# Where a position table is cast during attention, and how its products are ordered, in a two-layer image kernel

## The chip, the cores and the metric

The kernel runs on one core of a Trainium2 chip. The metric is device time in microseconds (us) of one execution. Three runs of the kernel before gave 2399.17, 2401.52 and 2405.88; their median, 2401.52, is the time before.

The engines are named as in the profile: PE (TensorE, the matrix products; PEld are its weight loads), DVE (VectorE), ACT (ScalarE), POOL (GpSimd) and SP (SyncE, which here issues DMAs only).

## The reference

Eight images of 32 x 32 tokens with 384 channels go through two layers. Layer 0 is group normalisation, attention with six heads of 64 channels over the 1,024 tokens of an image, a projection and a residual. To the logits it adds relative positions, taken apart into rows and columns:

```
attn  = einsum('bqd,bkd->bqk', q * SCALE, k)
rel_h = einsum('bhwc,hkc->bhwk', r_q, Rh)      # r_q: q as (heads, 32, 32, 64)
rel_w = einsum('bhwc,wkc->bhwk', r_q, Rw)
attn  = attn(b, h, w, h', w') + rel_h[..., None] + rel_w[..., None, :]
out   = softmax(attn) @ v @ proj_w + proj_b
```

Layer 1 is a layer norm with causal single-head attention and a residual, and then a feed-forward: a layer norm, a matrix of signs, a quantisation to 8 bits (clip of `y * 128 / (max|y| + eps)`) over a group of images, gelu, another matrix of signs, another such quantisation, and a residual. Eight images in five groups make groups of one image, so images 0 to 4 pass through the feed-forward and images 5 to 7 get zeros from it.

## The kernel before

**Order of the work.** The images are done one after the other in the order 5, 0, 1, 2, 3, 4, 6, 7. Each engine executes its own list of instructions, one after the other. A scheduler makes these lists when the program is built: it starts from the order of the Python code and may move work forward whose inputs and buffers are there earlier. The helper `tc.issue_after(ins)` keeps what is issued inside its block behind the instruction `ins`. PSUM tiles come from a pool of eight banks (`o_tile`), pages in SBUF from a pool of twelve (`page`) and larger tiles from a pool of eleven (`image`, `flat`).

**Start of an image, `layer0`.** Six calls of `queries_keys(m)` make q (m = 0 to 2, one for each pair of heads) and k (m = 3 to 5). Each is two halves of three 128x512 matmuls (`f_qk`, L438); ACT takes the first half out of PSUM (L468), DVE the second (L466). The table products belong to q: `positions(p)` multiplies q of pair p with the relative table (`f_rel`, L484, two halves of two matmuls); ACT copies the row part out of PSUM (L489), DVE the column part (L490); SP writes both to DRAM (`far`, L496) and reads them back as a shifted table of the pair (`near`, L501). In the kernel before, `positions(m - 1)` follows `queries_keys(m)` for m = 1, 2 and 3, so that a product, a projection, a product, a projection alternate. After m = 3 the last piece of the previous image's feed-forward is issued (`unfinished.pop()()`, the function `finish`), and then come k of pairs 1 and 2 and the eight tiles of v (`f_v`, L534; ACT and DVE copy them out, L537).

An image that follows one with a feed-forward (five do: 1, 2, 3, 4 and 6) has its first two projections, m = 0 and m = 1, computed ahead of time, inside that feed-forward (`ahead`, `project_qk`). Its start is therefore `f_rel` and `f_qk` of m = 2. The end of the feed-forward lies beside it: DVE finds the scale `qs` and the limits `qu` and `ql` (L946, L948), POOL clips eight tiles (L950), and DVE adds them scaled to `f_x` (L954, eight); these additions are part of `finish`, so in the Python code they follow m = 3 and `positions(2)`.

**Casting a table, `place(p)`.** The shifted table of a pair is split into a rounded part and a remainder so that the matmul can use both: ACT casts (`hi`, L514), DVE subtracts (`lo`, L515), twice each per pair (rows, then columns). Sixteen DMAs then put the parts into the four operands `r` (L522), eight of them issued by SP (`hi`) and eight by POOL (`lo`). In the kernel before `place` is a generator with one stop, between rows and columns. `place(0)` runs whole before attention; `place(1)` and `place(2)` are drawn from the generator `others` within attention.

**Attention, `attend0_fast`.** Six rounds go through (p, half) = (0,0), (0,1), (1,0), (1,1), (2,0), (2,1). In a round

- PE makes eight tiles of scores, each from two products q k (L590) and two products of a unit matrix with `r` (L594);
- ACT takes two exponentials of each tile (L600);
- DVE adds the eight tiles up, once L605 and six times L607 (`add_up`), then transposes and reduces (`over_tiles`, L624, L626);
- PE multiplies the exponentials with v (`f_av`, L615), and ACT copies the result out (L662);
- for the round before, PE makes the denominators (`f_den`, L633), DVE takes reciprocals (L637), sums both for a check on the values (`seen`, L427, L428; the last readers of the PSUM bank) and spreads them (L641, L642), and POOL multiplies (L659). This stands behind the sixth addition of DVE (`late_add`, `adds[4]`).

In the third round (1,0) `residual` loads the image again (SP, L106) and POOL adds a bias to its eight tiles (L569). In rounds 1 and 2 (p = 0) the kernel before draws two steps each from `later`, which puts a whole `place` into each of them:

```
if p == 0:
    with tc.issue_after(last_exp[0]):
        for _ in range(2):
            next(later, None)
```

Here `last_exp[0]` is the last exponential of the round on ACT; the subtractions on DVE are issued in the same block.

**First image only.** Image 5 also prepares the feed-forward's weights: `binarize`, called in round 5, loads them in pieces (POOL's DMAs, L232), and DVE sums them (L250). The scheduler moves the start of this forward: in the trace the first load is issued at 99.98 and the first sum starts at 106.6, ahead of the third round.

Of the kernel before, what the change touches and what calls it, by code (L numbers as in the profile page):

```python
# [11 lines left out]
F32 = mybir.dt.float32  # L12
# [3 lines left out]
ALU = mybir.AluOpType  # L16
# [9 lines left out]
NPAIR = NH // 2  # L26
# [49 lines left out]
def conv_attn_hybrid(  # L76
# [19 lines left out]
    nc = tc.nc  # L96
# [197 lines left out]
    def multiply_out(pools):  # L294
        both = pools.flat("wqkT")
        wqT_sb, wkT_sb = (both[:, i * NC * C : (i + 1) * NC * C].rearrange("p (k c) -> p k c", k=NC) for i in range(2))
        nc.sync.dma_start(out=wqT_sb, in_=wqT.rearrange("(k p) c -> p k c", p=P))
        nc.sync.dma_start(out=wkT_sb, in_=wkT.rearrange("(k p) c -> p k c", p=P))
        for m in range(NC):
            ps = pools.o_tile(f"wqk_{m}")  # L300
            for k in range(NC):
                nc.tensor.matmul(ps[:, :C], wqT_sb[:, k, ts(m, P)], wkT_sb[:, k, :], start=(k == 0), stop=(k == NC - 1))
            nc.vector.tensor_scalar_mul(wqk[:, m, :], ps[:, :C], C**-0.5)

    def stages(pools):
# [137 lines left out]
        def layer0(b, xT):  # L443
# [9 lines left out]
            def queries_keys(m):  # L453
                p = m % NPAIR
                bias = bqk[:, m : m + 1]
                made = ahead.pop((b, m)) if (b, m) in ahead else project_qk(b, xT, m)
                for half, ps in enumerate(made):
                    t = ts(half, 512)
                    if m < NPAIR:
                        dst = q[:, p, t]  # L460
                    else:
                        dst = k[:, p, t].rearrange("d (g n i) -> d g i n", n=2, i=P)
                        ps = ps.rearrange("d (g i n) -> d g i n", n=2, i=P)
                    scale = qscale if m < NPAIR else 1.0
                    if half:
                        nc.vector.tensor_scalar(dst, ps, scale, bias, ALU.mult, ALU.add)  # L466
                    else:
                        nc.scalar.activation(dst, ps, AF.Identity, bias=bias, scale=scale)  # L468
# [5 lines left out]
            def positions(p):  # L474

                if p < 1:
                    *pages, near = (pools.page(f"{n}_{b}_{p}") for n in ("far0", "far1", "near"))
                else:
                    room = pools.flat(f"far_{b}_{p}")
                    *pages, near = (room[:, ts(i, T)] for i in range(3))  # L480
                for half in range(2):
                    ps = [pools.o_tile(f"rel_{b}_{p}_{half}_{par}") for par in range(2)]
                    for par in range(2):
                        nc.tensor.matmul(  # L484
                            ps[par], rel[rows[par]].rearrange("d a n -> d (a n)"), q[rows[par], p, ts(half, 512)],
                            start=True, stop=True,
                        )
                    for par in range(2):
                        nc.scalar.copy(pages[par][:HD, ts(half, 512)], ps[par][:HD])  # L489
                        nc.vector.tensor_copy(  # L490
                            pages[par].rearrange("i (w h) -> i w h", h=H)[HD:, :, ts(half, H // 2)],
                            ps[par][HD:].rearrange("i (h w) -> i w h", w=W),
                        )
                for par in range(2):
                    far = store.tile([P, T], F32, tag=f"far_{p}_{par}", bufs=2, name=f"{pools.path}_far_{b}_{p}_{par}")
                    nc.sync.dma_start(out=far, in_=pages[par])  # L496
                    start = far[0:1, 0:1]
                    for d in range(2):
                        for half in range(2):
                            at, step = (d * HD + (half if d else 16 * half)) * T, (2 if d else 1) * T  # L500
                            nc.sync.dma_start(  # L501
                                out=near[ts(4 * d + 2 * half + par, 16)].rearrange("m (n o) -> m n o", n=32),
                                in_=bass.AP(start.tensor, start.offset + at, [[step, 16], [T + 32, 32], [1, 32]]),
                            )
                return near, [page.bitcast(F32R) for page in pages]

            def place(p, near, pages):


                for d in range(2):  # L510
                    hi, lo, src = (t[ts(d, HD)].rearrange("k (h w) -> k h w", h=H) for t in (*pages, near))
                    if d:
                        src = near[ts(d, HD)].rearrange("k (w h) -> k h w", h=H)
                    nc.scalar.copy(hi, src)  # L514
                    nc.vector.tensor_tensor(lo, src, hi.bitcast(F32), ALU.subtract)  # L515
                    if d == 0:
                        yield
                for part in range(4):
                    for d in range(2):
                        for i in range(2):  # L520
                            half = part % 2 if d else part // 2
                            (nc.gpsimd if i else nc.sync).dma_start(  # L522
                                out=r[part][:, p, :].bitcast(F32).rearrange("(m i) t -> i m t", i=4)[2 * i + d],
                                in_=pages[i][ts(2 * d + 1 - half, 32)].bitcast(F32),
                            )
# [13 lines left out]
            near = []  # L539
            for m in range(2 * NPAIR):  # L540
                queries_keys(m)
                if 0 < m <= NPAIR:
                    near.append(positions(m - 1))
                if m == NPAIR and unfinished:
                    unfinished.pop()()

                    early = pools.small.tile([P, 1], F32, tag="early", name=f"early0_{b}")
                    nc.scalar.activation(early, k[:, 0, T - 1 :], AF.Exp, scale=0.0)
            for j in range(NJ):
                values(j)  # L550
            r.extend(pools.image(f"r_{b}_{part}", F32R) for part in range(4))
            for _ in place(0, *near[0]):
                pass

            def others():
                for p in range(1, NPAIR):
                    yield from place(p, *near[p])
                    yield

            later = others()  # L560
            for _ in () if pools.fast else later:
                pass
            if pools.fast and b == ORDER[0]:
                join_biases(pools)

# [8 lines left out]
        def attend0_fast(residual, b, q, k, r, v, later):  # L574
# [5 lines left out]
            last_exp, last_matmul = [None], [None]  # L580
# [22 lines left out]
            def add_up(p, half, prs):  # L603
                total = pools.page(f"sum0_{b}_{p}_{half}")
                adds = [nc.vector.tensor_tensor(total, prs[0], prs[1], ALU.add).ins]  # L605
                for pr in prs[2:]:
                    adds.append(nc.vector.tensor_tensor(total, total, pr, ALU.add).ins)  # L607
                return total, adds[4]

            def values(p, half, prs):  # L610
                av = pools.o_tile(f"av0_{b}_{p}_{half}")
# [34 lines left out]
            for p, half in itertools.product(range(NPAIR), range(2)):  # L646
                t, last = ts(half, 512), (p, half) == (NPAIR - 1, 1)
                prs = [scores(p, c, half) for c in range(NJ)]
                if b == ORDER[0] and (p, half) == (0, 0):
                    multiply_out(pools)  # L650
                if b == ORDER[0] and (p, half) == (2, 0):
                    signs.append(binarize(pools))
                    next(signs[0])
                total, late_add = add_up(p, half, prs)
                if waiting is not None:
                    p0, t0 = waiting[0], ts(waiting[1], 512)
                    with tc.issue_after(late_add):
                        rb = reciprocals(*waiting)
                    (nc.vector if last else nc.gpsimd).tensor_tensor(oT[:, p0, t0], oT[:, p0, t0], rb, ALU.mult)  # L659
                av = values(p, half, prs)  # L660
                if not last:
                    nc.scalar.copy(oT[:, p, t], av)  # L662
                if (p, half) == (1, 0):
                    xt = residual()
                if p == 0:
                    with tc.issue_after(last_exp[0]):
                        for _ in range(2):
                            next(later, None)
                waiting = (p, half, over_tiles(p, half, total))
            nc.vector.tensor_tensor(oT[:, p, t], av, reciprocals(*waiting), ALU.mult)  # L670
            with behind_last():
# [334 lines left out]
    with ExitStack() as scope:  # L1006
        pools = Pools(scope, tc, "f")
# [43 lines left out]
```

## Time and profile before

| | us |
|---|---|
| time before, median of three runs | 2401.52 |
| profiled execution, its own time | 2400.84 |
| profiled execution, span from first to last instruction | 2399.1 |
| mean granted TensorE clock in it | 0.992 |
| L590, q k scores: 1536 matmuls | 423.8 busy, 27.3 idle before |
| L607, additions: 288, mean 1311 ns | 377.4 busy, 17.8 idle before |
| L514, casts: 32, mean 1532 ns | 49.0 busy, 0.8 idle before |
| L515, subtractions: 32, mean 1770 ns | 56.6 busy, 47.5 idle before |
| L490, DVE's copies of products: 96, mean 692 ns | 61.8 busy, 13.1 idle before |
| L569, POOL's bias additions: 64, mean 1728 ns | 108.8 busy, 50.0 idle before |

How to read this: "busy" is the sum over all instructions of that line; "idle before" is the time in which the engine stood just before one of them. Idle time of an engine counts only if the chain that sets the end passes through it. Each line of code has one row for each engine and shape, so a row's count tells over how many images or rounds it is spread: 32 subtractions are four for each image, those of pairs 1 and 2; those of pair 0 stand in a row of their own.

The profile gives times in microseconds from the start of the span. In its tables of stretches, a row holds the stretch, its length, then the busy time of PE, PEld, DVE, ACT and POOL with the number of instructions, the granted clock, the DMA share and GB/s.

### The profile page before, as it was taken

The page shows a single profiled execution, that of the slowest core. Times are in us where ns is not written, and L with a number is a line of the kernel's source. Part 1 is how long each engine was busy: PE and PEld are TensorE (multiplying, and loading weights), DVE is VectorE, ACT ScalarE, POOL GpSimd, SP SyncE. Part 2 cuts the span into 40 slices and gives each one's busy share as a digit, 9 for nine tenths or more (in the row PEclk, how much of TensorE's full clock was granted, in tenths as well). Part 3 has the DMA queues.
Part 4 walks back from the last instruction along what each step waited for, and adds up shares of the span by engine and source line. Part 5 has one row for each costly group of instructions (what it writes and reads, how often), then busy time and mean ns, then how long its engine had stood idle before and what let it go on. Part 6 is the DMA issues. An engine that isn't in the chain of part 4 may idle for free.

```text
span 2399.1 us, 26120 instructions
## 1 busy us (share of the span) xinstructions
PE 2347.1 (98%) x9442; PEld 1311.2 (55%) x9442; DVE 1441.9 (60%) x2302; ACT 1041.7 (43%) x1763; POOL 329.9 (14%) x421
## 2 busy tenths in 40 slices
PE   7899999999999999999999999999999999999998
PEld 3445544558644577445684455864457744554454
DVE  4585558655587347684455864558734668524851
ACT  3451155227463246551375522746424655115520
POOL 0310014000240001410002300024000131001300
PEclk9999999999999999999999999999999999999999
DMA  6610371220631012510108211053101271017100
GB/s 165 191 39 25 151 145 47 79 79 1 141 97 66 1 40 83 145 43 34 40 4 174 60 66 40 1 133 105 53 14 40 69 151 44 1 50 153 36 1 28
DMA packets 154795, 169.99 MB, mean 71 GB/s; under 512 B 113408, under 2 KB 126048, under 8 KB 153120
## 3 DMA queue, kind: packets, MB, share of 16 engines
q1 hardware_dynamic: 134416, 98.93, 16.4%
q0 software_dynamic: 17184, 69.22, 9.7%
q8 instruction: 77, 1.26, 0.2%
q10 hardware_dynamic: 3056, 0.08, 0.1%
q14 instruction: 62, 0.51, 0.1%
HBM read 75.38 MB, written 42.47 MB: 49 GB/s over the span
## 4 chain that ended last, share of the span: by engine, by line
PE 90%; DVE 5%; DMA 3%; SPq 1%; issue 1%; ACT 0%; POOL 0%; DVEq 0%; ACTq 0%
PE f_s L590 12%; PE f_av L615 11%; PE f_qk L438 10%; PE f_s L779 8%; PE f_av L792 8%; PE f_y L940 7%; PE f_y L899 7%; PE f_pj L386 5%; PE f_v L386 5%; PE f_q L738 5%; PE f_v L534 5%; PE f_s L594 4%; DVE f_sum L607 3%; PE f_rel L484 2%; DMA f_x<-in_x 1%; PE f_pt L314 1%
## 5 line engine op out<-in xcount | busy, mean ns | idle before, releaser
L600 ACT ACTIVATE f_pr<-f_s 128x512 f32<-128x512 f32 x768 | 413.5, 595 | 103.7 <-PE f_s L594 87.4
L590 PE MATMUL f_s<-f_q,f_k 64*128 64x512 f32 x1536 | 423.8, 611 | 27.3 <-DVE seen L427 27.3
L607 DVE TENSOR_TENSOR f_sum<-f_sum,f_pr 128x1024 f32<-128x1024 f32 x288 | 377.4, 1311 | 17.8 <-ACT f_pr L600 0.9
L615 PE MATMUL f_av<-f_pr,f_v 128*64 128x512 f32 x1536 | 339.3, 594 | 0.0
L594 PE MATMUL f_s<-f_r,unit 64*128 64x512 f32 x768 | 329.2, 808 | 0.2 <-DMA f_r<-f_far 0.2
L438 PE MATMUL f_qk<-f_gnT,wqkv_sb 128*128 128x512 f32 x576 | 257.3, 599 | 1.5 <-DVE f_gnT L349 1.5
L590 PEld LDWEIGHTS f_s<-f_q,f_k 64*128 64x128 f32 x1536 | 159.7, 191 | 157.5 <-issue 66.0
L615 PEld LDWEIGHTS f_av<-f_pr,f_v 128*64 128x64 f32 x1536 | 106.3, 137 | 196.4 <-issue 192.4
L779 PE MATMUL f_s<-f_q,f_lnT 128*128 128x512 f32 (+3 forms) x576 | 195.9, 488 | 0.0
L792 PE MATMUL f_av<-f_v,f_pr 128*128 128x385 f32 x576 | 195.3, 486 | 0.0
L438 PEld LDWEIGHTS f_qk<-f_gnT,wqkv_sb 128*128 128x128 f32 x576 | 108.0, 191 | 143.1 <-issue 131.1
L786 ACT ACTIVATE f_pr<-f_s 128x512 f32<-128x512 f32 (+3 forms) x96 | 47.1, 491 | 263.7 <-DVE f_s L784 217.6
L522 POOL DMA_DIRECT2D f_r<-f_far x192 | 102.6, 537 | 377.7 <-DVE f_far L515 343.9
L792 PEld LDWEIGHTS f_av<-f_v,f_pr 128*128 128x128 f32 x576 | 108.2, 190 | 77.3 <-issue 11.5
L779 PEld LDWEIGHTS f_s<-f_q,f_lnT 128*128 128x128 f32 x576 | 102.0, 190 | 77.8 <-issue 54.1
L594 PEld LDWEIGHTS f_s<-f_r,unit 64*128 64x128 f32 x768 | 86.6, 192 | 86.7 <-issue 83.1
L903 ACT ACTIVATE f_h<-f_y,b_sb 128x256 f32<-128x256 f32 x240 | 100.9, 471 | 67.3 <-PE f_y L899 67.3
L910 DVE TENSOR_REDUCE am<-f_h 128x1 f32<-128x1024 f32 (+2 forms) x80 | 71.6, 947 | 96.2 <-ACT f_h L903 96.2
L738 PE MATMUL f_q<-f_lnT,wqk 128*128 128x512 f32 x288 | 127.5, 592 | 0.0
L386 PE MATMUL f_pj<-wproj_sb,f_oT 128*128 128x384 f32 x384 | 127.3, 488 | 0.0
L386 PE MATMUL f_v<-wv_sb,f_lnT 128*128 128x384 f32 x384 | 126.5, 486 | 0.0
L534 PE MATMUL f_v<-wqkv_sb,f_gnT 128*128 128x384 f32 x384 | 125.1, 486 | 0.0
(153 smaller groups left out, 3036.0 us busy)
## 6 DMA issues: line engine op xcount, KB each, us to landing
f_far<-f_far SPq DMA_DIRECT2D x48, 512.0 KB, 3.2
f_r<-f_far POOLq DMA_DIRECT2D x192, 128.0 KB, 3.8
f_r<-f_far SPq DMA_DIRECT2D x192, 128.0 KB, 3.2
f_gnT<-in_xT SPq DMA_DIRECT2D x24, 512.0 KB, 4.6
f_x<-in_x SPq DMA_DIRECT2D x32, 384.0 KB, 6.4
out_y<-f_x POOLq DMA_DIRECT2D x28, 384.0 KB, 4.4
f_far<-f_far SPq DMA_DIRECT2D x128, 64.0 KB, 4.9
f_w1a<-w1s POOLq DMA_DIRECT2D x5, 1536.0 KB, 7.0
```

Source lines behind the costliest of these rows:

```text
L386: nc.tensor.matmul(ps[:, :C], xT[:, k, ts(j, P)], w[:, k, cols], start=(k == 0), stop=(k == NC - 1))
L438: nc.tensor.matmul(made[half], wqkv_sb[:, i, ts(m, P)], xT[:, i, ts(half, 512)], start=(i == 0), stop=(i == NC - 1))
L534: nc.tensor.matmul(ps, keys[:, i, j // 2, j % 2], wqkv_sb[:, i, 2 * C :], start=(i == 0), stop=(i == NC - 1))
L590: nc.tensor.matmul(sc[par], k[rows[par], p, ts(c, P)], q[rows[par], p, ts(half, 512)], start=True, stop=False)
L594: last_matmul[0] = nc.tensor.matmul(sc[par], unit[rows[par], c // 2 % 2].rearrange("i h w -> i (h w)"), r[2 * (c // 4) + c % 2][rows[par], ...
L600: last_exp[0] = nc.scalar.activation(pr[:, ts(par, 512)], sc[par], AF.Exp).ins
L607: adds.append(nc.vector.tensor_tensor(total, total, pr, ALU.add).ins)
L615: last_matmul[0] = nc.tensor.matmul(av[ts(par, HD), :], v[:, c, ts(2 * p + par, HD)], pr[:, ts(par, 512)], start=(c == 0), stop=(c == NJ - 1),
L738: nc.tensor.matmul(ps, wqk[:, k, ts(m, P)], xT[:, half, k, :], start=(k == 0), stop=(k == NC - 1))
L779: nc.tensor.matmul(sc[:, lo:], xT[:, c // 4, k, ts(c % 4, P)], q[:, half, k, lo:], start=(k == 0), stop=(k == NC - 1),)
L792: nc.tensor.matmul(av[:, : C + 1], prs[c][:, ts(j - c, P)], v[:, c, :], start=(c == 0), stop=(c == j))
L899: nc.tensor.matmul(ps, w1k[i // 2][:, ts(m, P)], xs[i % 2][:, half, i // 2, :], start=(i == 0), stop=(i == 2 * NC - 1))
```

## The change

Two things change, both in `layer0` and `attend0_fast`.

1. `place` is no generator any more. It is called whole, with `behind`, a pair of instructions: its casts (ACT) are issued after the first, its subtractions (DVE) after the second. In attention, `place(1)` is called in round 1 (p = 0, half 0) and `place(2)` in round 3 (p = 1, half 0), instead of rounds 1 and 2, with the round's last exponential for the casts and its last addition (`adds[-1]`) for the subtractions. `add_up` returns its additions for this.
2. `positions(0)` and `positions(1)` both follow `queries_keys(1)`, and `positions(2)` follows `queries_keys(2)`, instead of one after each of m = 1, 2, 3. So the table product of pair 2 also comes one projection earlier.

No instruction is added or taken away.

```diff
-            def place(p, near, pages):
+            def place(p, near, pages, behind=(None, None)):
+
+                def after(ins):
+                    return contextlib.nullcontext() if ins is None else tc.issue_after(ins)
 
                 for d in range(2):
                     hi, lo, src = (t[ts(d, HD)].rearrange("k (h w) -> k h w", h=H) for t in (*pages, near))
                     if d:
                         src = near[ts(d, HD)].rearrange("k (w h) -> k h w", h=H)
-                    nc.scalar.copy(hi, src)
-                    nc.vector.tensor_tensor(lo, src, hi.bitcast(F32), ALU.subtract)
-                    if d == 0:
-                        yield
+                    with after(behind[0]):
+                        nc.scalar.copy(hi, src)
+                    with after(behind[1]):
+                        nc.vector.tensor_tensor(lo, src, hi.bitcast(F32), ALU.subtract)
                 for part in range(4):
...
             for m in range(2 * NPAIR):
                 queries_keys(m)
-                if 0 < m <= NPAIR:
-                    near.append(positions(m - 1))
+                if m == 1:
+                    near.extend(positions(p) for p in range(2))
+                if m == 2:
+                    near.append(positions(2))
                 if m == NPAIR and unfinished:
                     unfinished.pop()()
...
-            for _ in place(0, *near[0]):
-                pass
-
-            def others():
-                for p in range(1, NPAIR):
-                    yield from place(p, *near[p])
-                    yield
-
-            later = others()
+            place(0, *near[0])
+
+            def later(p, *behind):
+                place(p, *near[p], behind)
+
...
-                return total, adds[4]
+                return total, adds
...
-                    with tc.issue_after(late_add):
+                    with tc.issue_after(adds[4]):
                         rb = reciprocals(*waiting)
...
-                if p == 0:
-                    with tc.issue_after(last_exp[0]):
-                        for _ in range(2):
-                            next(later, None)
+                if half == 0 and p + 1 < NPAIR:
+                    later(p + 1, last_exp[0], adds[-1])
                 waiting = (p, half, over_tiles(p, half, total))
```

More of the change, by code (lines that the diff above doesn't have):

```diff
@@ L551, in layer0 @@
             r.extend(pools.image(f"r_{b}_{part}", F32R) for part in range(4))
-            for _ in place(0, *near[0]):
-                pass
-            def others():
-                for p in range(1, NPAIR):
-                    yield from place(p, *near[p])
-                    yield
-            later = others()
-            for _ in () if pools.fast else later:
-                pass
+            place(0, *near[0])
+            def later(p, *behind):
+                place(p, *near[p], behind)
+            for p in () if pools.fast else range(1, NPAIR):
+                later(p, None, None)
             if pools.fast and b == ORDER[0]:
@@ L653, in attend0_fast @@
                     next(signs[0])
-                total, late_add = add_up(p, half, prs)
+                total, adds = add_up(p, half, prs)
                 if waiting is not None:
                     p0, t0 = waiting[0], ts(waiting[1], 512)
-                    with tc.issue_after(late_add):
+                    with tc.issue_after(adds[4]):
                         rb = reciprocals(*waiting)
```

## The prediction

> **What bounds the kernel now.** I read the page's engine list first, then the waits by engine, then the timelines of the stretches that the change touches.
>
> ```profile
> PE 2347.1 (98%) x9442; PEld 1311.2 (55%) x9442; DVE 1441.9 (60%) x2302; ACT 1041.7 (43%) x1763; POOL 329.9 (14%) x421
> ```
>
> TensorE (PE) is the bound nearly everywhere: a microsecond is won or lost only where PE stands or runs slowly. PE's waits name one place:
>
> ```profile
> PE f_s L590 <- DVE seen L427: 27.3, 8, 8.2
> ```
>
> Eight waits, one for each image, all in the third round of layer-0 attention: a score matmul wants the PSUM slot of the denominator tile, which VectorE (DVE) frees with L427. Why DVE is late shows in one image's rounds (round 1 starts at 656.06, round 2 at 672.00, round 3 at 688.06):
>
> ```profile
> 660.99 1.22 DVE L607 TENSOR_TENSOR f_sum<-f_sum,f_pr 128x1024 f32<-128x1024 f32 x1
> 667.28 1.22 DVE L515 TENSOR_TENSOR f_far<-f_far 64x1024 fp32r<-64x1024 f32 x1 [5.06 <-ACT f_far L514]
> ...
> 683.26 1.53 DVE L515 TENSOR_TENSOR f_far<-f_far 64x1024 fp32r<-64x1024 f32 x1 [1.65 <-DMA f_x<-in_x]
> ...
> 686.76 2.60 DVE L515 TENSOR_TENSOR f_far<-f_far 64x1024 fp32r<-64x1024 f32 x1
> ...
> 695.05 0.16 DVE L427 TENSOR_REDUCE seen<-f_den 128x1 f32<-128x16 f32 x1
> ```
>
> The position subtractions (L515) stand amid the additions, and each waits for a ScalarE cast that comes after the round's last exponential: 5.06 and 1.65 us of idle, with additions ready behind it. What it costs PE:
>
> ```profile
> 688.06:709.71 21.65, 18.84 (x86) 9.74 (x84) 21.15 (x23) 9.25 (x17) 13.42 (x13) 0.92 0.29 77
> 709.71:725.80 16.09, 16.09 (x88) 7.06 (x86) 15.29 (x20) 9.22 (x17) 2.25 (x2) 1.00 0.01 2
> ```
>
> A clean round takes 16.07; this one 21.65, at a granted clock of 0.92 (the column after POOL's). From one f_av start to the next, the excess over 16.07 in the eight images is 11.88 (first), 6.57, 5.58, 3.64, 6.97, 5.33, 5.85 and 3.86: 49.7 in all, 37.8 without the first.
>
> The other stretch is the start of an image that follows a feed-forward (five images):
>
> ```profile
> 613.64 1.99 PE L484 MATMUL f_rel<-f_q,rel 64*128 64x512 f32 x8
> 615.56 5.42 PE L438 MATMUL f_qk<-f_gnT,wqkv_sb 128*128 128x512 f32 x12
> 620.90 1.99 PE L484 MATMUL f_rel<-f_q,rel 64*128 64x512 f32 x8
> ```
>
> ```profile
> 621.01 0.75 DVE L466 TENSOR_SCALAR f_q<-f_qk,bqk 128x512 f32<-128x512 f32 x1 [2.17 <-PE f_qk L438]
> 623.63 1.56 DVE L954 SCALAR_TENSOR_TENSOR f_x<-f_y,qs,f_x 128x384 f32<-128x384 f32 x2 [1.87 <-POOL f_y L950]
> ```
>
> ```profile
> 622.95 6.11 POOL L950 TENSOR_SCALAR f_y<-f_y,qu,ql 128x384 f32<-128x384 f32 x8 [7.41 <-PE f_rel L484]
> ```
>
> PE has no gap there, because q of pair 2 (L466) leaves PSUM before DVE meets the previous image's last additions (L954), which wait for POOL's clips (L950). POOL's idle is put down to PE's f_rel, but in the five images the clip starts 1.4 to 2.1 us after that product begins, not at a fixed distance; its stated inputs are the limit `ql` (L948, 617.37) and a feed-forward matmul long done.
>
> [...] L950 has such an instruction at 615.5, and the clip starts 7.4 us later, 5.4 after `ql`. So the clips don't come earlier when the products do. [...] 0.82 to 1.00 granted in the eight third rounds.
>
> **The change, part by part.**
>
> *Subtractions behind the last addition (L515, L514).* In round 1, DVE adds without a stop: L605 at 659.66, seven additions at 1.25 to 668.5, two subtractions (1.22 + 1.92; their casts end at 669.3) to 671.7, transpose and reduction to 674.1 instead of 679.1. Round 2 holds no subtraction: from 675.7 five additions to 681.9, then two beside POOL's bias additions (L569, 682 to 696, 1.95 each): L427 at 684 instead of 695, when PE needs it by 692.4. Round 3 takes pair 2's subtractions after its L427: 691.7 + 6.9 + 0.2 + 1.3 = about 700, needed by 708; with the subtractions DVE ends near 708, when round 4's first additions come in. Pair 2's table is cast by 706, its eight POOL DMAs (0.53 each, 3.8 to land) are in by about 714; round 5 reads at 720.7. SP keeps its order of DMAs; POOL now puts the eight L569 ahead of pair 2's DMAs. Everything fits with 6 us to spare: **-37.8** in seven images (at worst -33).
>
> *First image.* DVE also sums the weights (L250) there and waited 11.9 us for them. POOL's order in the changed program puts all eight L569 ahead of the first weight DMA, where four stood: issue at 106.5 instead of 99.98, landing (6.6) at 113 instead of 106.6. But two additions now stand before the first sum and the rest between sums: 113.2 + 3 x 0.72 + 4 x 1.21 + 0.25 gives L427 at 120.5, against 120.81: nothing won. Ten further sums now stand ahead of round 3's additions and wait for the next weight DMAs, which wait for sum five (126.7): landed (5.1 and 7.0) by 134.4, additions from 136.4, L427 at 144.2, while PE needs it at 140.5: 3.7 plus a clock loss. **+6** (bounds -1 and +10).
>
> *Products of pairs 0 and 1 in a row.* The PE work is the same: four matmuls, 1.92 us, move. Images without a feed-forward before them: q of pair 2 is out of PSUM 0.85 us after its last matmul, the first half of pair 2's product takes 0.96: **0**, covered by that half; uncovered, 0.85 in each of three images. After a feed-forward DVE's order becomes: four copies of pair 1, **seven L954**, then L466 of pair 2's second half. PE's next matmuls, pair 2's second half, wait for this L466, and all of k and v is queued behind them. Counted from the first f_rel: clip 1 starts at 9.0 (mean of five images, 8.7 to 9.3), ends at 9.65; six further pairs of clip and L954 at 0.985 (from the trace: 1.97 for two) give 15.55; the seventh L954 0.6, L466 0.75, handoff 0.05: 16.95. PE would be there at 2 x 1.92 + 5.35 + 0.96 = 10.15. Standing: 6.8. Bounds: clips at their bare 0.645 give 4.7, full alternation at 1.2 gives 8.1. After such a gap PE runs slowly. From length and clock of the third rounds the loss is 0 to 3.5, with the long gap included about 2.6 of useful time; I take 2.6 [...]. 5 x (6.8 + 2.6) = **+47** (23.5 to 57.5).
>
> Sum: 2399.1 - 37.8 + 6 + 47 = 2414.3 span. The profiled run took 1.7 more than its span (2400.84), and lies 0.7 below the median of 2401.5: **2416.5**.
>
> **The rivals.**
> - *Waits beside each other* (faster, crosses to the other side): DVE doesn't stand, because the clips are ready when pair 2's projection ends, i.e. POOL starts them by 617.5 and not by 623. For: the release by f_rel which the profile names would move them 3.4 us earlier. Against: the varying distance, the inputs. Then 2401.5 - 37.8 + 6 = 2370. It decides once the clips start 5 us earlier.
> - *Short stand at full clock:* 4.7 each and no clock loss: 2401.5 - 37.8 + 6 + 23.5 = 2393. For: two of the eight third rounds stayed at 1.00 after 2.5 us. Against: a gap of 7 us, twice as long.
> - *The rounds don't recover:* the stand moves into round 4, since round 3 now holds subtractions and part of POOL's additions: 2401.5 + 6 + 47 = 2455. Against: 6 us of room.
>
> **How the numbers follow.** My forecast has 0.78, with its own range 2405 to 2428; the first rival 0.06, the short stand 0.08, no recovery 0.08. The range 2400 to 2430 holds most of the forecast and little else. 0.3% is 7.2 us, about what a measurement of this kernel can tell from no change: the bounds are 2394 and 2409. Faster: 0.06 + half of the short stand, 0.10. Same: the other half and 0.10 of the forecast's low end, 0.14. Slower: 0.76.
>
> **What would show it.** PE's waits: L590 on L427 gone from seven images, left in the first; new, five waits of f_rel on DVE's L466, some 6 to 8 us each, with a clock below 1 behind them. DVE: seven L954 in a row on POOL's clips, then L466. Clips still 9 us after the first f_rel. Rounds 3 at 16.1. In the first image a gap in round 4. I am wrong if f_rel doesn't wait, or if the third rounds keep their excess.

## The result and the profile after

| | before | after |
|---|---|---|
| median, us | 2401.81 (six runs, the three named above among them, 2399.17 to 2405.88) | 2412.70 (six runs, 2411.66 to 2414.12) |
| profiled execution, us | 2400.84 | 2412.40 |
| its span, us | 2399.1 | 2410.3 |
| ratio of the times, with 95% interval | | 1.0046 (1.0033 to 1.0059) |

The change makes the kernel 10.9 us slower: it wins what it set out to win and loses more in another place. In the page of the kernel after, the engine list comes first (busy time, share of the span, instructions):

```profile
PE 2337.5 (97%) x9442; PEld 1293.9 (54%) x9442; DVE 1430.1 (59%) x2302; ACT 1042.0 (43%) x1763; POOL 320.8 (13%) x421
```

PE is 9.6 us less busy than before in a span that is 11.2 us longer, so it stands for longer. Its waits in the kernel after (total, times, longest) say where:

```profile
PE f_rel L484 <- DVE f_q L466: 35.4, 5, 7.6
PE f_s L590 <- DVE seen L427: 13.0, 2, 6.9
```

Of the eight waits for L427, seven are gone; the first image's is left, and that image has a second one. The first line is new: five waits, one for each image that follows a feed-forward. The stretches from the first table product to the first product with v show what such an image costs. First the kernel before, then the kernel after, for the same image (stretch, length, busy time of PE, PEld, DVE, ACT and POOL, clock, DMA share, GB/s):

```profile
613.64:664.99 51.35, 51.35 (x170) 25.05 (x169) 26.69 (x40) 23.76 (x38) 13.77 (x21) 1.00 0.71 164
```

```profile
613.28:674.36 61.08, 53.51 (x170) 25.72 (x170) 29.01 (x43) 23.93 (x38) 15.32 (x21) 0.92 0.63 138
```

PE was busy for the whole stretch before. After, it stands for 61.08 - 53.51 = 7.57 us, and is busy for 2.16 us longer with the same matmuls, at a mean clock of 0.92.

DVE's timeline of the kernel after shows what the copy L466 is queued behind (start, duration, line, operation, count; in brackets the idle time before the first of them and what ended it):

```profile
617.18 3.73 DVE L490 COPY f_far<-f_rel 64x512 f32<-64x512 f32 x6
623.47 1.56 DVE L952 SCALAR_TENSOR_TENSOR f_x<-f_y,qs,f_x 128x384 f32<-128x384 f32 x2 [2.56 <-POOL f_y L948]
625.43 0.62 DVE L952 SCALAR_TENSOR_TENSOR f_x<-f_y,qs,f_x 128x384 f32<-128x384 f32 x1 [0.40 <-POOL f_y L948]
...
629.50 0.62 DVE L952 SCALAR_TENSOR_TENSOR f_x<-f_y,qs,f_x 128x384 f32<-128x384 f32 x1 [0.40 <-POOL f_y L948]
630.15 0.75 DVE L466 TENSOR_SCALAR f_q<-f_qk,bqk 128x512 f32<-128x512 f32 x1
```

PE's timeline of the same kernel and time:

```profile
616.91 5.42 PE L438 MATMUL f_qk<-f_gnT,wqkv_sb 128*128 128x512 f32 x12
622.26 1.13 PE L484 MATMUL f_rel<-f_q,rel 64*128 64x512 f32 x4
630.96 2.08 PE L484 MATMUL f_rel<-f_q,rel 64*128 64x512 f32 x4 [7.57 <-DVE f_q L466]
```

The input of L466 was complete at about 622.3, when the projection ended. DVE stood idle just then (2.56 us, waiting for POOL's first clip), but it took its list in order: the seven additions that stand ahead of L466, each waiting for its clip, went first, and L466 started at 630.15. After the wait PE needs 2.08 us for four matmuls that otherwise take about one (the eight of one pair took 1.99). The stretches just after the wait, in the next image, give the clock:

```profile
955.49:959.90 4.41, 4.41 (x7) 1.67 (x8) 3.07 (x5) 1.06 (x2) 2.55 (x4) 0.50 0.76 268
959.90:965.00 5.10, 5.10 (x13) 2.28 (x12) 0.86 (x1) 2.44 (x2) 0.00 (x0) 1.00 1.12 238
```

For 4.4 us PE is granted half the clock (0.50), which is 2.2 us of lost work, and then the full one (1.00).

The first image's rounds three and four in the kernel after:

```profile
101.54:127.51 25.97, 19.05 (x89) 10.02 (x89) 12.89 (x17) 9.46 (x18) 7.69 (x9) 0.87 0.18 64
127.51:152.19 24.68, 18.05 (x89) 7.97 (x87) 19.51 (x27) 12.58 (x21) 5.23 (x7) 0.86 0.37 114
```

Before, round three took 27.95 and round four 16.05. So round three gained 1.98 and round four lost 8.63. DVE's timeline of the kernel after shows the sums of the weights (L250) that wait for their loads, and the two L427 that come late behind them:

```profile
112.82 0.79 DVE L250 TENSOR_REDUCE sums_w<-f_w 128x1 f32<-128x614 f32 x1 [13.53 <-DMA f_w<-in_w1T]
...
119.66 0.17 DVE L427 TENSOR_REDUCE seen<-f_den 128x1 f32<-128x16 f32 x1
...
130.68 1.99 DVE L250 TENSOR_REDUCE sums_w<-f_w 128x1 f32<-128x307 f32 x5 [4.95 <-DMA f_w<-in_w1T]
134.14 1.98 DVE L250 TENSOR_REDUCE sums_w<-f_w 128x1 f32<-128x304 f32 x5 [1.47 <-DMA f_w<-in_w2T]
136.03 1.22 DVE L605 TENSOR_TENSOR f_sum<-f_pr,f_pr 128x1024 f32<-128x1024 f32 x1
...
143.81 0.17 DVE L427 TENSOR_REDUCE seen<-f_den 128x1 f32<-128x16 f32 x1
```

Round lengths below are taken in the same way, from the first `f_av` of one round to the first of the next; the start of an image goes from its first `f_rel` to its first `f_av`. The account of the span:

| part | us |
|---|---|
| third rounds of seven images, 21.47 to 16.06 on average | -37.9 |
| start of five images after a feed-forward, 51.45 to 60.45 on average | +45.0 |
| first image, rounds three and four | +6.65 |
| start of the images without a feed-forward before them, 3 x 0.36 | -1.1 |
| from the last image's sixth `f_av` to the end (114.75 to 113.38) and small differences between images | -1.5 |
| sum, the two spans | +11.2 |

### The profile page after: what moved, and what is told of

Read it like the earlier page. It is cut to its first block, busy times and chain, and to the rows that moved or that the text cites. A ratio compares the mean times of both kernels' runs of the same rounds, so it can differ in the third digit from the quotient of the medians.

```text
span 2410.3 us, 26183 instructions
## 1 busy us (share of the span) xinstructions
PE 2337.5 (97%) x9442; PEld 1293.9 (54%) x9442; DVE 1430.1 (59%) x2302; ACT 1042.0 (43%) x1763; POOL 320.8 (13%) x421
## 4 chain that ended last, share of the span: by engine, by line
PE 93%; DVE 3%; POOL 2%; DMA 1%; issue 1%; ACT 0%; SPq 0%; DVEq 0%; POOLq 0%; ACTq 0%
PE f_s L590 13%; PE f_av L615 12%; PE f_qk L438 10%; PE f_s L777 8%; PE f_av L790 8%; PE f_y L938 7%; PE f_y L897 7%; PE f_pj L386 5%; PE f_v L386 5%; PE f_v L536 5%; PE f_q L736 5%; PE f_s L594 3%; PE f_rel L484 2%; PE f_pt L314 1%; POOL f_y L948 1%; DVE f_sum L607 1%
## 5 line engine op out<-in xcount | busy, mean ns | idle before, releaser
L590 PE MATMUL f_s<-f_q,f_k 64*128 64x512 f32 x1536 | 403.4, 599 | 13.0 <-DVE seen L427 13.0
L607 DVE TENSOR_TENSOR f_sum<-f_sum,f_pr 128x1024 f32<-128x1024 f32 x288 | 364.3, 1265 | 22.4 <-DVE rt L637 0.6
L594 PE MATMUL f_s<-f_r,unit 64*128 64x512 f32 x768 | 310.9, 796 | 0.0
L438 PE MATMUL f_qk<-f_gnT,wqkv_sb 128*128 128x512 f32 x576 | 261.4, 610 | 1.5 <-DVE f_gnT L349 1.5
L590 PEld LDWEIGHTS f_s<-f_q,f_k 64*128 64x128 f32 x1536 | 147.1, 187 | 142.7 <-issue 75.2
L438 PEld LDWEIGHTS f_qk<-f_gnT,wqkv_sb 128*128 128x128 f32 x576 | 111.1, 196 | 148.3 <-issue 134.3
L594 PEld LDWEIGHTS f_s<-f_r,unit 64*128 64x128 f32 x768 | 76.4, 188 | 90.3 <-issue 89.8
```

The source lines that it names most:

```text
L438: nc.tensor.matmul(made[half], wqkv_sb[:, i, ts(m, P)], xT[:, i, ts(half, 512)], start=(i == 0), stop=(i == NC - 1))
L590: nc.tensor.matmul(sc[par], k[rows[par], p, ts(c, P)], q[rows[par], p, ts(half, 512)], start=True, stop=False)
L594: last_matmul[0] = nc.tensor.matmul(sc[par], unit[rows[par], c // 2 % 2].rearrange("i h w -> i (h w)"), r[2 * (c // 4) + c % 2][rows[par], ...
```

## The experiments

In the variants the code lines shift by a few: the table's casts and products, the clips and the last additions carry numbers a few away from those of the kernel they come from. The first four variants were measured beside a median of about 2404 for the kernel before, the others beside 2401, so medians of different variants compare to some 3 us; the ratios and the round lengths compare better.

| kernel | first image, rounds 3 and 4 | start after a feed-forward, mean of five | third round, mean of the other seven | median us |
|---|---|---|---|---|
| before | 27.95, 16.05 | 51.45 | 21.47 | 2401.8 |
| after | 25.97, 24.68 | 60.45 | 16.06 | 2412.7 |
| casts moved, products as before | 25.58, 23.97 | 51.42 | 16.06 | 2371.3 |
| products in a row, casts as before | 28.15, 16.08 | 61.10 | 22.01 | 2446.9 |
| after, additions behind q | 25.88, 24.08 | 51.01 | 16.06 | 2366.2 |
| after, no second reduction | 26.21, 23.73 | 56.68 | 16.06 | 2393.1 (one run) |
| casts moved, sums late | 16.05, 16.05 | 51.37 | 16.06 | 2353.8 |
| casts behind the additions, rounds 1 and 2 | 28.62, 17.78 | 51.36 | 16.06 | 2364.7 |
| casts among the additions, rounds 1 and 3 | 25.37, 16.18 | 51.36 | 16.06 | 2362.2 |
| after, additions behind q and sums late | 16.08, 16.09 | 51.01 | 16.06 | 2351.7 |

The first question was whether the gain belongs to one half of the change and the loss to the other.

### The casts alone

```diff
-                if m == 1:
-                    near.extend(positions(p) for p in range(2))
-                if m == 2:
-                    near.append(positions(2))
+                if 0 < m <= NPAIR:
+                    near.append(positions(m - 1))
```

> The changed kernel with the table products one after each of m = 1, 2, 3 again; the casts stay behind the last addition, in rounds 1 and 3. My theory (the stand after a feed-forward belongs to the order of the products alone, the recovery of the third rounds to the casts alone): PE's waits of f_rel on L466 are gone, the third rounds of seven images stay at 16.1, and the first image keeps its two gaps: 2401.8 - 37.8 + 6.6 = about 2371. Rival (the stand comes from the moved casts or their DMAs): the five waits stay and the time is 2410 or more.

Measured 2371.31, ratio to the kernel before 0.9863 (0.9845 to 0.9881). The waits for L466 are gone, and of those for L427 the first image's two are left:

```profile
PE f_s L588 <- DVE seen L427: 12.3, 2, 6.9
```

The rival falls: the moved casts have no part in the stand after a feed-forward.

### The products alone

The kernel before with the calls of `positions` as in the change.

> The kernel before with the table products of pairs 0 and 1 in a row; the casts as before. My theory: the third rounds keep their 37.8 us of excess and the five stands of 9 us come on top: 2401.8 + 45 - 1 = about 2446, within 7 for what the first image does. Rival (a stand at the start of an image gives DVE and POOL a lead which takes away part of the third round's excess, so that the two don't add): 2415 to 2430.

Measured 2446.95, ratio 1.0166 (1.0140 to 1.0192). Both kinds of wait lie beside each other:

```profile
PE f_rel L484 <- DVE f_q L466: 35.9, 5, 7.8
PE f_s L592 <- DVE seen L427: 28.0, 8, 8.1
```

The third rounds keep their excess (22.01 against 21.47), so the lead that DVE and POOL get while PE stands takes nothing from it. The two parts are independent as far as the intervals tell: -1.37% and +1.66% alone make +0.29%, against +0.46% (0.33 to 0.59) together.

This part of the change again holds two things: the products of pairs 0 and 1 in a row, and the product of pair 2 directly behind its own projection. In the kernel before, a whole projection of 5.4 us (m = 3) lies between; by an estimate from these lengths alone it would cover most of a stand of 7 us. The two weren't run apart.

### The last additions behind the copy of q

```diff
                     else:
-                        nc.vector.tensor_scalar(dst, ps, scale, bias, ALU.mult, ALU.add)
+                        out = nc.vector.tensor_scalar(dst, ps, scale, bias, ALU.mult, ALU.add).ins
+                        if m == 2:
+                            evicted.append(out)
...
-            near = []
+            near, evicted = [], []
...
-                    unfinished.pop()()
+                    with tc.issue_after(evicted[0]):
+                        unfinished.pop()()
```

> The changed kernel with the previous image's last additions (L952) put behind DVE's copy of q of pair 2 (L466), all else the same. My theory (PE stands because that copy is queued behind seven additions that wait for POOL's clips): the five waits of f_rel on L466 are gone, 2412.7 - 45 = about 2368. Rival (two products in a row stand by themselves, for PSUM banks or for DVE's eight copies): at most 10 us are won, 2403 to 2413.

Measured 2366.17, ratio 0.9840 (0.9822 to 0.9857). DVE's timeline of this kernel, in the same image:

```profile
621.82 0.75 DVE L466 TENSOR_SCALAR f_q<-f_qk,bqk 128x512 f32<-128x512 f32 x1 [1.46 <-PE f_qk L438]
622.48 1.46 DVE L955 SCALAR_TENSOR_TENSOR f_x<-f_y,qs,f_x 128x384 f32<-128x384 f32 x2
623.97 1.30 DVE L492 COPY f_far<-f_rel 64x512 f32<-64x512 f32 x2
```

Now DVE waits for PE and not PE for DVE, the additions find their clips done, and the start takes 51.01. Two products in a row don't make PE stand: with them, and with the rest of the change, the kernel is 46.5 us faster by the medians, and 47.4 by the profiled spans, of which the five starts make 47.2. What made it stand was the place of seven additions in DVE's list.

### Why the clips come when they come

The profile puts POOL's idle time ahead of its first clip (L948 after) down to PE in one image and to nothing in four. To test in their place whether it comes from the reduction just ahead, behind which POOL executes its configuration instructions (MODIFY_POOL_CONFIG, two at 615.1 behind a reduction at 614.83; in the kernel before two at 615.5, with the first clip at 622.95), this kernel leaves out the maximum over the partitions in the second quantisation:

```diff
-            nc.gpsimd.partition_all_reduce(ga, g, P, bass_isa.ReduceOp.max)
+            if name[0] == "2":
+                nc.vector.tensor_copy(ga, g)
+            else:
+                nc.gpsimd.partition_all_reduce(ga, g, P, bass_isa.ReduceOp.max)
```

> The changed kernel in which the second quantisation's maximum over the partitions is left out (each partition takes its own maximum by a copy on DVE), so that POOL executes no partition reduction just ahead of its clips. My theory [...]: the first clip starts within 1 us of ql, 5 to 6 us earlier; the stand falls from 7.1 to about 3.4 us, and the time to 2386 to 2394. Rival (POOL waits for PE or for data, as the named releaser says): the clips start as late as before and the time stays within 3 of 2412.

Measured 2393.11 in one run. POOL's timeline of this kernel, DVE's and PE's:

```profile
617.40 5.80 POOL L951 TENSOR_SCALAR f_y<-f_y,qu,ql 128x384 f32<-128x384 f32 x8 [40.56 <-PE f_rel L484]
```

```profile
622.73 3.52 DVE L955 SCALAR_TENSOR_TENSOR f_x<-f_y,qs,f_x 128x384 f32<-128x384 f32 x6
626.28 0.75 DVE L466 TENSOR_SCALAR f_q<-f_qk,bqk 128x512 f32<-128x512 f32 x1
```

```profile
627.09 2.08 PE L484 MATMUL f_rel<-f_q,rel 64*128 64x512 f32 x4 [3.64 <-DVE f_q L466]
```

`ql` starts at 617.06; the first clip follows 0.34 us later, where in the kernel after it followed 5.8 us later (617.00 to 622.79). The two MODIFY_POOL_CONFIG instructions, which stood at 615.1 just behind the reduction, now execute at 576.8, during the feed-forward, where nothing waits for them. The projection L438, which the profile names in the kernel after, runs on to 622.3 here, five microseconds past the first clip. So PE isn't what the clips wait for; without a reduction just ahead they start 0.34 us after `ql`. What POOL does in the 5.8 us of the kernel after is not shown. The stand halves, to 18.2 us in five, and is not gone, because six additions still stand ahead of L466. The scheduler also put two of the eight additions among the copies here, so the 3.6 us are not the earlier clips' alone.

### The first image's sums

The kernel with the casts alone, with `summed[0]` set to a round's last addition in attention, and in layer 1:

```diff
                 for work in 2 * signs:
-                    next(work, None)
+                    with tc.issue_after(summed[0]):
+                        next(work, None)
```

> The kernel with the casts moved and the products as before (2371.3), and in the first image all sums of the weights (L250) put behind DVE's last addition of the sixth round. My theory (these sums, and the weight loads that they wait for, are all of the first image's two gaps): its third and fourth rounds fall from 25.6 and 24.0 to 16.1, 2371.3 - 17.4 = about 2354. Rival (the sums come just as dear in layer 1, or the third round is late for POOL's bias additions as well): 2361 to 2371.

Measured 2353.79, ratio 0.9802 (0.9783 to 0.9820). The two rounds in this kernel:

```profile
102.19:118.25 16.06, 16.06 (x89) 6.81 (x89) 15.62 (x15) 9.21 (x18) 11.46 (x8) 1.00 0.28 98
118.25:134.30 16.05, 16.05 (x88) 6.80 (x88) 15.52 (x17) 12.23 (x20) 7.06 (x9) 1.00 0.51 133
```

With the casts moved, all of the first image's excess is sums of weights that stand ahead of additions while their load is on its way. In the kernel before DVE stood for a load as well:

```profile
106.63 3.59 DVE L250 TENSOR_REDUCE sums_w<-f_w 128x1 f32<-128x614 f32 x5 [11.92 <-DMA f_w<-in_w1T]
```

How much of that kernel's 11.88 us of excess is the sums' and how much the subtractions' was not run apart. The twenty sums now start at 174.6 instead of 112.8, and none of them waits for a load. In layer 1, where DVE now takes them between its normalisations, PE waits 1.7 us for two normalised tiles, which it doesn't do with the casts alone.

### Which half of the cast change is needed

First the rounds as before, with the subtractions behind the last addition; then rounds 1 and 3, with the subtractions free among the additions. Both with the products as before.

```diff
-                if half == 0 and p + 1 < NPAIR:
-                    later(p + 1, last_exp[0], adds[-1])
+                if p == 0:
+                    later(half + 1, last_exp[0], adds[-1])
```

> As the kernel with the casts moved and the products as before (2371.3), but pair 2's casts in round 2 again, behind its last addition. My theory (a subtraction does harm only where it stands ahead of additions that are ready): DVE's seen (L427) still comes before PE wants it in the third round of seven images, about 2371, at most 2375. Rival (pair 2 must leave round 2, because DVE has too much in rounds 2 and 3 together): part of the 37.8 comes back, 2380 to 2400.

Measured 2364.70, ratio 0.9846 (0.9827 to 0.9864).

```diff
-                    later(p + 1, last_exp[0], adds[-1])
+                    later(p + 1, last_exp[0], None)
```

> The other half alone: pair 2's casts in round 3, but the subtractions of both pairs not held behind the last addition, so that they stand among the additions again; products as before. My theory: round 1 ends 5 us late on DVE as before, but round 2 has no subtraction and makes it up, and in round 3 the idle ahead of the subtractions fits into what is left before round 4: 0 to 1.5 us of excess in each of seven images, 2371 to 2382. Rival (idle of DVE ahead of a subtraction always reaches PE): 5 us each, now in the fourth round, 2395 to 2410.

Measured 2362.17, ratio 0.9837 (0.9818 to 0.9855). DVE's timeline in this second kernel shows the subtraction's old wait in round 1, and what becomes of it:

```profile
658.92 1.22 DVE L519 TENSOR_TENSOR f_far<-f_far 64x1024 fp32r<-64x1024 f32 x1 [5.06 <-ACT f_far L517]
...
680.94 0.16 DVE L427 TENSOR_REDUCE seen<-f_den 128x1 f32<-128x16 f32 x1
```

The 5.06 us are the same as in the kernel before, but round 2 makes up for them: L427 of the third round comes 8.2 us after the start of the round's stretch (672.72), where before, with pair 2's subtractions in round 2, it came 14.0 us after it (695.05 from 681.07) and PE stood. The fourth round takes 16.17 instead of 16.06: 0.1 an image, at the low end of what was expected.

Either half alone clears the third rounds of the seven images. Both kernels lie below the kernel with both halves (2371.3), and below what was expected. The intervals of their ratios still overlap with that kernel's, but the profiled spans agree (3.7 and 7.3 us shorter), and so does the place, which neither theory named: in the first image round four takes 17.78 and 16.18, where with both halves it takes 23.97. In the first of them POOL issues the second load only at 133.0, and just one of the ten further sums stands ahead of round four's L427 (142.40), at which PE doesn't stand. In the second the ten further sums find their weights landed (first sum at 107.4, with no load waited for after it), since POOL issues the first load between its bias additions, as before the change.

### Both repairs

The changed kernel with the additions behind q and the sums late.

> The changed kernel with both repairs: the previous image's last additions behind the copy of q of pair 2 (2366.2 by itself), and the sums of the weights behind the sixth round of the first image. My theory: the two lie in different places and add up, 2366.2 - 17.8 = about 2348. Rival (the sums come just as dear in layer 1): 2356 to 2366.

Measured 2351.66 (five runs, 2350.26 to 2353.84), ratio 0.9793 (0.9776 to 0.9809): nearly all of the expected gain, 14.5 of 17.8 us. 1.7 of the rest are again the two waits in layer 1 (the third line); the other 1.6 is not accounted for:

```profile
PE f_gmean L336 <- DVE gmv L333: 10.8, 1, 10.8
PE f_bad L201 <- DVE worst L199: 1.9, 1, 1.9
PE f_pt L314 <- DVE f_xn L376: 1.7, 2, 1.4
```

This is the fastest kernel run, 50 us below the one before. Against the kernel with the casts alone and the sums late (2353.79) its interval overlaps, so whether products in a row are worth anything here can't be told from the times.

## Why the prediction was right

The forecast was slower, 2416.5 in a range of 2400 to 2430; it measured 2412.7. Step by step:

- **Subtractions behind the last addition, -37.8.** Measured -37.9 in the kernel after; the casts alone show that it is theirs. L427 comes 2.98 us after the start of the third round's stretch (693.43 from 690.45); the predicted 684 is 2.9 after the start of the same stretch before, at 681.07. The prediction read the change as one measure; the runs show that it holds two, each sufficient.
- **First image, +6.** Measured +6.65. "Nothing won" in round three was wrong by 2 us, with the first sum at 112.82 (113 predicted) and L427 at 119.66 (120.5). In round four L427 came at 143.81 (144.2); PE wanted its slot at 138.1 and not at 140.5, since round three had ended earlier, so it stood 6.06 and not 3.7. The two differences nearly cancel, so that the sum came out at +6.65 is in part luck. That the sums are the cause of both gaps in the changed kernel is shown by the runs with the sums late.
- **Products in a row, +47.** Measured 45.0. The stand was 7.08 us on average (35.4 in five) for 6.8; the clips started 8.8 to 9.5 after the first product for 9.0. That the additions' place in DVE's list is what PE pays for is shown by the run that moves them. The clock's part was 9.0 + 0.36 - 7.08 = 2.3 for 2.6: the stretch of 4.4 us at 0.50 shown above. The 0.82 among the prediction's clocks is the first image's, where PE stood 8.17 us. In the other seven third rounds of the kernel before it stood 2.49 to 3.09 us at 0.85 to 1.00, without order: 0.85 with the wait of 2.49, 1.00 with one of 2.75. The 2.6 was picked between such figures, so its closeness to 2.3 is in part luck. The upper bounds, 8.1 for the stand and 57.5 in all, were the author's estimate. In the kernel before a clip took 0.65 to 1.33 us and an addition L954 0.60 to 1.03; in the kernel after the eight clips of an image took 7.7. The rival in which the clips are ready early is excluded by the timeline. The run without the second reduction ties the late clips to that reduction: in the kernel after it is 7.0 to 7.7 us from the configuration to the first clip, 5.1 to 5.8 of them after `ql` starts (in the kernel before 6.8 to 7.4 and 5.0 to 5.6), and 0.34 after `ql` where the configuration could execute earlier.
- **Images without a feed-forward, 0.** Measured -0.36 each. In the trace of one of them, start to start, the products of pairs 0 and 1 take 3.64 us in a row and 3.83 apart, and the three projections of k 15.55 in a row and 15.76 with a product between. Both are shorter where the two kinds of matmul alternate less; what makes them shorter was not shown.
- **The sum.** 2414.3 predicted for the span, 2410.3 measured. (The step to the median, 1.7 and 0.7, makes 2416.7; 2416.5 was written.) The largest term of the difference is the five starts, 2 us; 1.4 lies in the last image's end, which no part of the change touches, and which varied between 113.4 and 114.8 in these profiles.

## What to carry to other kernels

Here a wait on one engine was paid by what was queued behind it: PE stood 7.08 us on average for a copy behind seven additions. So read a move as a change of each engine's list: the instruction that suffers can be one that the edit doesn't name, here a copy of q behind another image's additions. Where a producer can be late (here a load, with 13.53 us of idle time before the first sum, and POOL, with its first clip 5.1 to 5.8 us after `ql`), put the instructions that wait for it behind those that the bound engine is about to need, with an explicit order where a scheduler would decide otherwise. And test the halves of a change alone: here one was worth some 30 us and the other cost some 45, and the sum hid both.

## What was not expected of the hardware

The 7.0 to 7.7 us between POOL's configuration instruction and its first clip were counted on (7.4 in the kernel before); not expected was that the configuration executes early, at 576.8 instead of 615.1, once no reduction stands just ahead, so that the first clip starts 0.34 us after `ql`. In the kernel after the 7.0 to 7.7 us appear in no row of busy time and are put down to PE or to nothing as releaser.

And the clock loss grew less than the wait: with a wait of 3.64 us, at a mean granted clock of 0.97, the start of an image lost 56.48 - 51.01 - 3.64 = 1.8 us beside the wait itself; with 7.57 us, at 0.92, 61.08 - 51.01 - 7.57 = 2.5. These are two images of two kernels; no rule for other lengths follows.
